# Queries and keys of block attention by a seven-product block scheme, in a fused Macaron layer

## The chip, the cores and the metric

The kernel runs on one core of a Trainium2 chip. Its metric is the device time of one execution in microseconds (us). The kernel before was run three times: 1013.26, 1014.03 and 1014.54 us, median 1014.03 us. A further execution was taken with the hardware profiler; all durations below come from that one.

A core has four computing engines that run their own queues of instructions: TensorE (PE; its weight loads are shown apart as PEld), VectorE (DVE), ScalarE (ACT) and GpSimd (POOL). SyncE (SP) issues most of the transfers between the main memory and the core. An engine takes its instructions in the order in which they stand in its queue, and waits on semaphores where an operand is not there yet.

## The reference, cut to what matters

The layer takes 2048 tokens of 1024 features in float32 and does

```python
x = x + 0.5 * ffn(layernorm(x))      # routed scales, +-1 weights
x = x + attn(layernorm(x))
x = x + 0.5 * ffn(layernorm(x))
```

The attention is the part in which the change lies:

```python
x = conv1d(inputs, conv_w, taps=3, 1024 -> 768) + conv_b
q, k, v = split(x, 3)                             # 256 features each
# 16 blocks of 128 tokens
qh = einsum('btd,dhe->bthe', q, wq) + bq          # 16 heads of 64
kh = einsum('btd,dhe->bthe', k, wk) + bk
vh = einsum('btd,dhe->bthe', v, wv) + bv
scores = einsum('bqhe,bkhe->bhqk', qh * scale, kh), causal
o = softmax(scores) @ vh
out = (einsum('bqhe,hed->bqd', o, wo) + bo) @ proj_w + proj_b
```

For the queries, `wq` is a matrix of 256 x 1024; so is `wk` for the keys. The depth of 256 is two times the 128 rows of TensorE.

## The kernel before

**Stages.** The kernel runs five stages one after the other: the first feed-forward part (0 to about 215 us of the span), the convolution (to 453.9 us), the attention (to about 846 us, its end mixed with the start of the last part) and the second feed-forward part with the stores. The convolution is written as a minimal-filtering scheme over two halves of the tokens. For each half, `conv_ends` and then `conv_middle` go over six column blocks `w` of 128 output features. In `conv_middle`, each `w` has two product groups on TensorE (`cv`, tiles `cv_{half}_{w}_{0,1}`, each 32 matmul records of 128x256, L475). Their weights `u` (k = 1 to 4) are computed from the three taps `g` by VectorE in `taps` (L465 to L471). There is one buffer for each `k`, so the weights for `w+1` can only be written when the products of `w` that read that buffer are done, and the next product group cannot begin before its weights are there. VectorE then combines the results into `y4` (L540 to L549), which SP stores to `qkv_dram` (L550). Before `conv_middle(1)`, the program asks for the first group of q, k and v (`load_qkv(0)`, L667) and the weights `wv`, `wq`, `wk` (L668).

**Attention.** The tokens are taken in four groups `g` of 512 (four blocks of 128), and each group goes over eight pairs of heads `hp` (128 columns). That gives 32 steps `(g, hp)`, and five stages that are pipelined over steps: at turn `i` the program emits `stage_qkv` of step `i`, `stage_softmax` of step `i-1`, `stage_transpose` of `i-2`, `stage_values` of `i-3` and `stage_wo` of `i-4`.

- `stage_qkv` computes q and k of a pair of heads as a 128x512 block each: two accumulating matmuls over the two halves of depth (L732; a float32 matmul shows as two records), then one VectorE instruction that adds the bias and moves the block out of PSUM (L741, L743). At `hp` 0 and 4 it first computes the values of four pairs (L716; 16 records), moved out by ScalarE and VectorE in turn (L724, L726).
- `stage_softmax`: eight matmuls for the scores (`sc`, L753), a ScalarE copy (L763), a GpSimd causal select (L765), a VectorE maximum (L775), four exponentials with sums on ScalarE (L778), a reciprocal and a scaling on VectorE (L785, L786); all twice, for the two heads.
- `stage_transpose` (`pt`, L794), `stage_values` (`ao`, L807) and `stage_wo` (`acc`, L824) follow. `stage_proj` (`pp`, L843) comes once per group.

PSUM has two banks of 128x512 for each of four kinds. The kind `mm` serves the values, q and k, the projection and the feed-forward products.

**Order.** The text order gives the priority. A planner in the framework moves instructions against each other within each engine's queue by its own estimates, unless they are pinned (`pin`, `keep_in_program_order`) or stand in a manual part. So the queue order is fixed when the program is built, and the hardware follows it. The q, k, v loads of group `g+1` are issued at `hp` 0 of group `g`, into one pool of two buffers (`qkvp`). The residual rows `xr` are loaded at `hp` 1, get `proj_b` added by GpSimd (L709), and live in one ring of eight buffers (`rring`) that the rows `xf` of the second feed-forward part use too.

Of the kernel before, what the change touches and what calls it, by code (L numbers as in the profile page):

```python
# [9 lines left out]
F32 = mybir.dt.float32  # L10
# [3 lines left out]
ALU = mybir.AluOpType  # L14
# [3 lines left out]
P = 128  # L18
NB = 512
# [5 lines left out]
def kernel(  # L25
# [22 lines left out]
    nc = tc.nc  # L48
# [15 lines left out]
    def pool(stack, name, bufs, **kw):  # L64
        return stack.enter_context(tc.tile_pool(name=name, bufs=bufs, reuse_waits="tile", **kw))
# [36 lines left out]
    def pin(ins):  # L102

        tc.keep_in_program_order(ins)
# [524 lines left out]
    with ExitStack() as ph:  # L629
        work = pool(ph, "work1", 2, side="right")  # L630
        ffn = Ffn("f1", work, xnp, 0, NT, lambda t: x1[t], next_x, norm_x2, transpose_x2, beside)
        with tc.manual_schedule():
            begin(ffn, work)
        for dst, src in ((conv_b_sb, conv_b), (bq_sb, bq), (bk_sb, bk), (bv_sb, bv), (bo_sb, bo)):
            tc.keep_in_program_order(nc.gpsimd.dma_start(out=dst, in_=src))
        ffn.run()
# [13 lines left out]

    b2 = ctx.enter_context(ExitStack())
    aw = pool(b2, "aw", 1, side="right")
    qkvp = pool(b2, "qkvp", 2, side="right")
    qkvs = {}

    def load_qkv(g):
        qkvs[g] = qkvp.tile([P, NW, NB], F32, name=f"qkv_{g}", tag="qkv")
        half, at = divmod(g * NB, TH)
        for w in range(NW):
            nc.sync.dma_start(out=qkvs[g][:, w, :], in_=qkv_dram[half][w][:, ds(at, NB)])  # L660
# [6 lines left out]
    load_qkv(0)  # L667
    wv_sb, wq_sb, wk_sb = (load_rows(aw, a, n, HE) for a, n in ((wv, "wv_sb"), (wq, "wq_sb"), (wk, "wk_sb")))  # L668
    conv_middle(1, mp)
# [3 lines left out]
    b3 = ctx.enter_context(ExitStack())  # L673
    f2 = ctx.enter_context(ExitStack())
    rring = pool(b3, "rring", 8)
    rows, x3 = {}, {}

    def load_rows2(t):
        if t in rows:
            return  # L680
        rows[t] = rring.tile([P, D], F32, name=f"xf_{t}", tag="x")
        nc.sync.dma_start(out=rows[t], in_=x3[t])
# [4 lines left out]
    with ExitStack() as ph:  # L687
# [3 lines left out]
        load_qkv(1)  # L691
# [6 lines left out]
        vhs, qks, prs, pTs, oTs, accs = {}, {}, {}, {}, {}, {}  # L698

        def stage_qkv(g, hp):  # L700
            if hp == 0 and g > 0 and g + 1 < NG:
                load_qkv(g + 1)
            if hp == 1:
                for t in range(g * BPG, (g + 1) * BPG):
                    rows[t] = rring.tile([P, D], F32, name=f"xr_{t}", tag="x")
                    nc.sync.dma_start(out=rows[t], in_=x2[t])
            if 3 <= hp < 3 + BPG:
                xt = rows[g * BPG + hp - 3]
                pin(nc.gpsimd.tensor_tensor(xt, xt, projb_sb, ALU.add))  # L709
# [18 lines left out]
            got = []  # L728
            for n, (w_sb, first) in enumerate(((wq_sb, 0), (wk_sb, WC))):
                pq = bank("mm", [P, NB], f"pq_{g}_{hp}_{n}")  # L730
                for c in range(WC):
                    nc.tensor.matmul(  # L732
                        pq,
                        lhsT=w_sb[:, c, ts(hp, P)],
                        rhs=qkvs[g][:, first + c, :],
                        start=(c == 0),
                        stop=(c == WC - 1),
                    )
                h = ap2.tile([P, NB], F32, name=f"qk_{g}_{hp}_{n}", tag=f"qk{n}")
                if n == 0:  # L740
                    nc.vector.tensor_scalar(h, pq, bq_sb[:, hp : hp + 1], QSCALE, ALU.add, ALU.mult)  # L741
                else:
                    nc.vector.tensor_scalar(h, pq, bk_sb[:, hp : hp + 1], None, ALU.add)  # L743
                got.append(h)
            qks[g, hp] = got

        def stage_softmax(g, hp):
            qh, kh = qks.pop((g, hp))
# [88 lines left out]
        def stage_proj(g):  # L837
            o2T = accs.pop(g)
            for b in range(BPG):
                for h in range(NH2):  # L840
# [9 lines left out]
                    xt = rows[g * BPG + b][:, ts(h, NB)]  # L850
# [3 lines left out]
                nc.sync.dma_start(out=x3[t], in_=rows.pop(t))  # L854

        stages = (stage_qkv, stage_softmax, stage_transpose, stage_values, stage_wo)
        ended, parts = None, []
        for i in range(len(steps) + len(stages)):
            for n, stage in enumerate(stages):
                if 0 <= i - n < len(steps):  # L860
                    stage(*steps[i - n])
                if n == 0 and i == len(steps) - 1:

                    b2.close()
                    work = pool(f2, "work2", 2, side="right")
                    ffn = Ffn("f2", work, work, 0, NT, lambda t: rows[t], load_rows2, store, lambda t: None, lambda t: None)
                    parts = ffn.fill()
                if n == 1 and ended is not None:
                    stage_proj(ended)
                    ended = None  # L870
                if n in (1, 3) and i >= len(steps) and parts:
                    parts.pop(0)()
            last = i - (len(stages) - 1)
            if 0 <= last < len(steps) and steps[last][1] == NHP - 1:
                ended = steps[last][0]
# [5 lines left out]
    b3.close()  # L881
# [53 lines left out]
```

## Time and profile before

| What | Value |
|---|---|
| median of three runs | 1014.03 us |
| profiled execution, its own time | 1014.76 us |
| span of that execution | 1013.0 us |
| TensorE busy | 984.3 us (97%) |
| VectorE busy | 665.6 us (66%) |
| ScalarE / GpSimd busy | 388.4 / 239.4 us |
| attention groups 1, 2, 3 (480 to 768 us), each 96 us: TensorE / VectorE busy | 95.5 / 55.6, 95.9 / 53.6, 95.9 / 53.6 us |
| convolution, second half (332 to 456 us): TensorE / VectorE busy | 123.5 / 76.0 us of 124 |
| TensorE granted clock | 0.999 |

In a line of the profile, L732 is line 732 of the kernel; `out<-in` names the tiles, then come the shape and the number of records. In the groups by line, the first pair of numbers is the busy time in us and the mean duration of one record in ns; the second says how long the engine was idle just before, and who ended most of that idle time. In the lists in order of time, the first two numbers are the start and the duration in us, and square brackets give an idle time and its releaser. Matmuls overlap, so the distance between starts says what one costs in a stream, not its duration.

### The profile page before, as it was taken

The page shows a single profiled execution, that of the slowest core. Times are in us where ns is not written, and L with a number is a line of the kernel's source. Part 1 is how long each engine was busy: PE and PEld are TensorE (multiplying, and loading weights), DVE is VectorE, ACT ScalarE, POOL GpSimd, SP SyncE. Part 2 cuts the span into 40 slices and gives each one's busy share as a digit, 9 for nine tenths or more (in the row PEclk, how much of TensorE's full clock was granted, in tenths as well). Part 3 has the DMA queues.
Part 4 walks back from the last instruction along what each step waited for, and adds up shares of the span by engine and source line. Part 5 has one row for each costly group of instructions (what it writes and reads, how often), then busy time and mean ns, then how long its engine had stood idle before and what let it go on. Part 6 is the DMA issues. An engine that isn't in the chain of part 4 may idle for free.

```text
span 1013.0 us, 14588 instructions
## 1 busy us (share of the span) xinstructions
PE 984.3 (97%) x5420; PEld 694.8 (69%) x5420; DVE 665.6 (66%) x1243; ACT 388.4 (38%) x1074; POOL 239.4 (24%) x335
## 2 busy tenths in 40 slices
PE   5999999999999999999999999999999999899997
PEld 3778888888888888884555455545554555677776
DVE  4888887748978537756656545655565556767664
ACT  3566665410110110114445424533462552545440
POOL 3554543300000000002312211221031312543421
PEclk9999999999999999999999999999999999999999
DMA  8767554698643786217020041013003207756421
GB/s 248 221 179 210 177 169 133 226 360 294 217 158 125 226 297 213 94 46 287 1 63 1 11 156 63 1 63 104 1 1 124 73 12 208 187 147 164 106 83 63
DMA packets 39705, 139.68 MB, mean 138 GB/s; under 512 B 4617, under 2 KB 5641, under 8 KB 38610
## 3 DMA queue, kind: packets, MB, share of 16 engines
q1 hardware_dynamic: 34528, 121.65, 33.6%
q0 software_dynamic: 5088, 17.06, 9.0%
q8 instruction: 43, 0.70, 0.3%
q14 instruction: 28, 0.23, 0.1%
q10 hardware_dynamic: 18, 0.04, 0.0%
HBM read 81.84 MB, written 40.11 MB: 120 GB/s over the span
## 4 chain that ended last, share of the span: by engine, by line
PE 39%; issue 38%; DVE 10%; DMA 6%; POOL 6%; ACT 1%; POOLq 0%; DVEq 0%
PE pm_f L286 15%; PE cv L475 7%; PE ce L475 4%; POOL xr L709 3%; DMA xf<-x 3%; DMA out_dram<-xf 2%; PE pp L843 2%; PE tr_f L199 2%; DVE st_f L157 2%; POOL p L765 2%; PE acc L824 1%; PE tr L398 1%; PE lgp_f L207 1%; PE is_f L250 1%; PE pq L732 1%
## 5 line engine op out<-in xcount | busy, mean ns | idle before, releaser
L286 PE MATMUL pm_f<-sw,y_f 128*128 128x512 f32 x1024 | 265.4, 407 | 0.2 <-DVE x L296 0.2
L286 PEld LDWEIGHTS pm_f<-sw,y_f 128*128 128x128 f32 x1024 | 185.9, 190 | 40.6 <-DVE x L296 0.4
L475 PE MATMUL cv<-v,u 128*128 128x256 f32 x768 | 166.3, 379 | 0.3 <-DVE u L467 0.3
L475 PEld LDWEIGHTS cv<-v,u 128*128 128x128 f32 x768 | 145.8, 190 | 20.4 <-PE cv L475 0.7
L765 POOL TENSOR_SCALAR_AFFINE_SELECT p<-p 128x512 f32<-128x512 f32 x64 | 39.7, 644 | 507.8 <-ACT p L763 507.8
L778 ACT ACTIVATE p<-p,anm 128x128 f32<-128x128 f32 x256 | 99.0, 388 | 17.5 <-DVE anm L775 17.5
L264 POOL TENSOR_TENSOR y_f<-xnT_f,y_f 128x512 fp32r<-128x512 f32 x64 | 81.3, 1288 | 66.1 <-ACT y_f L263 65.3
L475 PE MATMUL ce<-v,g 128*128 128x256 f32 x384 | 84.3, 380 | 0.9 <-ACT m L489 0.9
L763 ACT COPY p<-sc 128x512 f32<-128x512 f32 x64 | 34.3, 588 | 127.6 <-PE sc L753 127.5
L475 PEld LDWEIGHTS ce<-v,g 128*128 128x128 f32 x384 | 72.4, 190 | 12.1 <-ACT m L489 2.3
L775 DVE TENSOR_REDUCE anm<-p 128x4 f32<-128x512 f32 x64 | 40.9, 680 | 49.5 <-POOL p L765 49.5
L824 PE MATMUL acc<-oT,wo_sb 128*128 128x512 f32 x128 | 67.7, 617 | 0.4 <-DVE oT L816 0.4
L295 DVE TENSOR_TENSOR pm_f<-pm_f,os_f 128x512 f32<-128x512 f32 x64 | 44.4, 693 | 27.9 <-PE pm_f L286 27.3
L732 PE MATMUL pq<-qkv,wq_sb 128*128 128x512 f32 x128 | 60.4, 593 | 0.0
L732 PE MATMUL pq<-qkv,wk_sb 128*128 128x512 f32 x128 | 60.1, 592 | 0.0
L843 PE MATMUL pp<-pw_sb,o2T 128*128 128x512 f32 x128 | 57.6, 600 | 0.4
L716 PE MATMUL pv<-wv_sb,qkv 128*128 128x512 f32 x128 | 56.5, 593 | 0.0
L778 ACT ACTIVATION_READ_ACCUMULATOR p<-p,anm 128x1 f32 x256 | 48.0, 187 | 0.0
L753 PEld LDWEIGHTS sc<-qk,qk 64*128 64x128 f32 x512 | 31.1, 187 | 23.7 <-issue 22.2
L786 DVE TENSOR_TENSOR p<-p,asum 128x512 f32<-128x512 f32 x64 | 45.6, 713 | 2.2
L200 ACT COPY xnT_f<-tr_f 128x512 f32<-128x512 f32 x60 | 32.5, 589 | 37.9 <-PE tr_f L199 36.1
L732 PEld LDWEIGHTS pq<-qkv,wk_sb 128*128 128x128 f32 x128 | 24.3, 190 | 30.6 <-issue 28.7
(134 smaller groups left out, 1440.9 us busy)
## 6 DMA issues: line engine op xcount, KB each, us to landing
g<-in_conv_w_dram SPq DMA_DIRECT2D x60, 512.0 KB, 4.1
win<-xw SPq DMA_DIRECT2D x16, 528.0 KB, 2.7
xl<-win SPq DMA_DIRECT2D x8, 1056.0 KB, 7.4
x<-in_x_dram SPq DMA_DIRECT2D x16, 512.0 KB, 3.8
x<-hbias POOLq DMA_DIRECT2D x16, 512.0 KB, 4.9
x<-x SPq DMA_DIRECT2D x16, 512.0 KB, 4.1
xr<-x SPq DMA_DIRECT2D x16, 512.0 KB, 6.5
x<-xr SPq DMA_DIRECT2D x16, 512.0 KB, 3.9
```

Of the source, the lines that this page charges most:

```text
L264: nc.gpsimd.tensor_tensor(yl, y, yh.bitcast(F32), ALU.subtract)
L286: nc.tensor.matmul(pm, lhsT=y[:, n, c, :], rhs=sw[:, c, ts(h, NB)], start=(c == 0 and n == 0), stop=(c == DC - 1 and n == 1),)
L295: nc.vector.tensor_tensor(pm, pm, o, ALU.mult)
L475: nc.tensor.matmul(acc.rearrange("p (t q) -> p t q", q=QT), lhsT=uk[:, c, :], rhs=V[half, k][:, :, c, :], start=(c == 0), stop=(c == DC - 1),)
L716: nc.tensor.matmul(pv, lhsT=qkvs[g][:, 2 * WC + c, ts(b, P)], rhs=wv_sb[:, c, ts(half, NB)], start=(c == 0), stop=(c == WC - 1),)
L732: nc.tensor.matmul(pq, lhsT=w_sb[:, c, ts(hp, P)], rhs=qkvs[g][:, first + c, :], start=(c == 0), stop=(c == WC - 1),)
L765: nc.gpsimd.affine_select(out=p, in_=p, pattern=[[0, BPG], [-1, P]], compare_op=ALU.is_ge, fill=NEG_INF, base=0, channel_multiplier=1,)
L775: nc.vector.tensor_reduce(nmax, p, AX.X, ALU.max, negate=True)
L778: nc.scalar.activation(p[:, b, :], p[:, b, :], AF.Exp, bias=nmax[:, b : b + 1], accum_out=asum[:, b : b + 1],)
L786: nc.vector.tensor_tensor(p, p, asum.unsqueeze(2).broadcast_to([P, BPG, P]), ALU.mult)
L824: nc.tensor.matmul(accs[g][m], lhsT=wo_sb[:, hp, ts(m, P)], rhs=oT, start=(hp == 0), stop=(hp == NHP - 1),)
L843: nc.tensor.matmul(pp, lhsT=o2T[:, m, ts(b, P)], rhs=pw_sb[:, m, ts(h, NB)], start=(m == 0), stop=(m == WC - 1),)
```

## The change

Before, q (or k) of two neighbouring pairs of heads `2m`, `2m+1` takes 2 x 2 = 4 matmuls of 512 columns, which is 8 block products of 128 x 128 by 128 x 256 tokens: two heads-pairs x two halves of tokens x two halves of depth. The change computes the same four blocks from seven such products, by Strassen's scheme in Winograd's form.

- `seven_weights` (once for `wq`, once for `wk`): four VectorE instructions build the sums of the weight blocks, in a new tile `s_q` or `s_k` and in place. Before it, ScalarE multiplies `wq` by the scale in place (two instructions), and GpSimd does so for `bq`. They stand before `conv_middle(1)` in the text.
- `seven_inputs` (for each group, once for q and once for k): four VectorE instructions of 128x256 build the sums of the token blocks, one of them in place in the loaded q, k, v tile.
- `seven` (one unit for each two steps and each of q, k): four products into two `mm` banks; a ScalarE copy and four VectorE instructions on what they gave; then three more products, written over the places that have been read, each followed by a VectorE instruction that adds it and the bias into the result. At an even `hp` the k unit of the current two steps runs, at an odd `hp` the q unit of the next two. The first q unit runs before the loop.
- The order of the stages within a turn is written out anew: loads, softmax, projection, values of v, first four products, `stage_wo`, the last three products, transpose, values.
- Pools: the two q, k, v buffers become two pools of one (`qkv0`, `qkv1`), and `qkv1` is taken after the memory of the convolution is given back. The residual rows get a ring of their own with five buffers (`aring`); the rows of the second feed-forward part get theirs (`rring`, eight) after the attention's memory is released. The rows `xr` are loaded at `hp` 5 instead of 1, and GpSimd adds `proj_b` at turn `i - 7`.

The diff, cut to its core:

```diff
+        tc.keep_in_program_order(nc.gpsimd.tensor_scalar(bq_sb, bq_sb, QSCALE, None, ALU.mult))
...
-    qkvp = pool(b2, "qkvp", 2, side="right")
+    qkv0 = pool(b2, "qkv0", 1, side="right")
...
+    def seven_weights(w_sb, name):
+        s = aw.tile([P, 3, NHP // 2, P], F32, name=f"s_{name}")
+        (a11, a21), (a12, a22) = (
+            [w_sb.rearrange("p c (n m e) -> p c n m e", m=2, e=P)[:, c, :, m, :] for m in range(2)] for c in range(2)
+        )
+        s1, s2, s4 = (s[:, n, :, :] for n in range(3))
+        nc.vector.tensor_tensor(s1, a21, a22, ALU.add)
+        nc.vector.tensor_tensor(s2, s1, a11, ALU.subtract)
+        nc.vector.tensor_tensor(a21, a11, a21, ALU.subtract)
+        nc.vector.tensor_tensor(s4, a12, s2, ALU.subtract)
+        return dict(p1=a11, p2=a12, p3=s4, p4=a22, p5=s1, p6=s2, p7=a21)
...
+    for c in range(WC):
+        nc.scalar.mul(wq_sb[:, c, :], wq_sb[:, c, :], QSCALE)
+    sevens = [seven_weights(w_sb, n) for w_sb, n in ((wq_sb, "q"), (wk_sb, "k"))]
     conv_middle(1, mp)
...
-    rring = pool(b3, "rring", 8)
...
+        qkv1 = pool(b2, "qkv1", 1, side="right")
+        tp = pool(b2, "tp", 1, side="right")
+        aring = pool(ph, "aring", 5)
+        load_qkv(1, qkv1)
...
+        def seven_inputs(g, n):
+            x = qkvs[g][:, n * WC : n * WC + 2, :].rearrange("p c (h t) -> p c h t", h=2)
+            (b11, b12), (b21, b22) = ([x[:, c, h, :] for h in range(2)] for c in range(2))
+            t = tp.tile([P, 3, NB // 2], F32, name=f"t_{g}_{n}", tag=f"t{n}")
+            t2, t3, t4 = (t[:, j, :] for j in range(3))
+            nc.vector.tensor_tensor(b12, b12, b11, ALU.subtract)
+            nc.vector.tensor_tensor(t2, b22, b12, ALU.subtract)
+            nc.vector.tensor_tensor(t3, t2, b11, ALU.subtract)
+            nc.vector.tensor_tensor(t4, b21, t2, ALU.subtract)
+            ts_[g, n] = dict(p1=b11, p2=b21, p3=b22, p4=t4, p5=b12, p6=t2, p7=t3)
+
+        def seven(g, pair, n):
...
+            xy, zv = (bank("mm", [P, 2, NB // 2], f"qk_{g}_{pair}_{n}_{j}") for j in range(2))
+            px, py, pz, pv = xy[:, 0, :], xy[:, 1, :], zv[:, 0, :], zv[:, 1, :]
...
+            for dst, p in ((px, "p1"), (py, "p6"), (pz, "p7"), (pv, "p5")):
+                product(dst, p)
+            nc.scalar.copy(c11, px)
+            nc.vector.tensor_tensor(c12, py, c11, ALU.add)
+            nc.vector.tensor_tensor(c21, pz, c12, ALU.add)
+            nc.vector.scalar_tensor_tensor(c22, pv, b2, c21, ALU.add, ALU.add)
+            nc.vector.tensor_tensor(c12, pv, c12, ALU.add)
+            yield
+            for dst, p, c, bias in ((px, "p2", c11, b1), (pz, "p4", c21, b2), (py, "p3", c12, b1)):
+                product(dst, p)
+                nc.vector.scalar_tensor_tensor(c, dst, bias, c, ALU.add, ALU.add)
+            yield
...
-            for n, (w_sb, first) in enumerate(((wq_sb, 0), (wk_sb, WC))):
-                pq = bank("mm", [P, NB], f"pq_{g}_{hp}_{n}")
-                for c in range(WC):
-                    nc.tensor.matmul(
...
-                if n == 0:
-                    nc.vector.tensor_scalar(h, pq, bq_sb[:, hp : hp + 1], QSCALE, ALU.add, ALU.mult)
-                else:
-                    nc.vector.tensor_scalar(h, pq, bk_sb[:, hp : hp + 1], None, ALU.add)
...
+        for n in range(2):
+            seven_inputs(0, n)
+        for _ in seven(0, 0, 0):
+            pass
...
+            at(stage_loads, 0)
...
+            at(stage_softmax, 1)
+            if i == len(steps):
+                b2.close()
+                rring = pool(f2, "rring", 8, side="right")
...
+            at(stage_v, 0)
+            unit = (stage_qk(i) if i < len(steps) else None) or iter(range(2))
+            next(unit)
+            at(stage_wo, 4)
+            next(unit)
+            at(stage_transpose, 2)
+            at(stage_values, 3)
+            if i < len(steps):
+                g, hp = steps[i]
+                if hp in (5, 6) and g + 1 < NG:
+                    seven_inputs(g + 1, hp - 5)
```

## The prediction

> **What bounds the kernel now.** I read the engines' busy shares first.
>
> ```profile
> PE 984.3 (97%) x5420; PEld 694.8 (69%) x5420; DVE 665.6 (66%) x1243; ACT 388.4 (38%) x1074; POOL 239.4 (24%) x335
> ```
>
> TensorE is the bound over the whole span, and VectorE is busy for two thirds. Next I read TensorE in order of time through one attention step without values.
>
> ```profile
> 501.19 1.16 PE L753 MATMUL sc<-qk,qk 64*128 64x128 f32 x16
> 502.28 1.09 PE L794 MATMUL pt<-ident,p 128*128 128x128 f32 x8
> 503.21 1.02 PE L824 MATMUL acc<-oT,wo_sb 128*128 128x512 f32 x2
> 504.17 1.09 PE L807 MATMUL ao<-pT,vh 128*64 128x128 f32 x16
> 505.19 1.12 PE L824 MATMUL acc<-oT,wo_sb 128*128 128x512 f32 x2
> 506.15 1.88 PE L732 MATMUL pq<-qkv,wq_sb 128*128 128x512 f32 x4
> 507.87 1.88 PE L732 MATMUL pq<-qkv,wk_sb 128*128 128x512 f32 x4
> 509.68 1.16 PE L753 MATMUL sc<-qk,qk 64*128 64x128 f32 x16
> ```
>
> No line has square brackets: TensorE never waits, and a step lasts 509.68 - 501.19 = 8.49 us. Eight 512-wide records take 506.15 to about 509.6, 3.43 us, 0.43 each. That is what the seven products replace.
>
> VectorE's list across the convolution's second half shows how little room that stage has.
>
> ```profile
> 374.63 1.23 DVE L465 TENSOR_TENSOR u<-g,g 128x1024 f32<-128x1024 f32 x1 [3.36 <-PE cv L475]
> 378.08 1.22 DVE L466 TENSOR_TENSOR u<-u,g 128x1024 f32<-128x1024 f32 x1 [2.23 <-PE cv L475]
> 379.56 1.22 DVE L467 TENSOR_TENSOR u<-u,g 128x1024 f32<-128x1024 f32 x1
> 381.70 1.22 DVE L469 SCALAR_TENSOR_TENSOR u<-g,g 128x1024 f32<-128x1024 f32 x1
> 384.99 1.22 DVE L470 SCALAR_TENSOR_TENSOR u<-g,u 128x1024 f32<-128x1024 f32 x1 [2.07 <-PE cv L475]
> ```
>
> The next weights wait in turn for products to free their buffers (the brackets), and are ready by 380.8, 4 us before TensorE wants them at 384.8, where the products that the last of these lines waits for are done. VectorE's idle time here is not free time in its queue. The transfers issued in the same microseconds (second number: KB; last: median us to landing):
>
> ```profile
> wq_sb<-in_wq_dram SPq DMA_DIRECT2D x1, 1024.0 KB, 10.3
> ```
>
> The seam to the attention, in order of time over all engines, and two later transfers:
>
> ```profile
> 453.85 7.03 PE L716 MATMUL pv<-wv_sb,qkv 128*128 128x512 f32 x16
> ...
> 457.00 0.62 DVE L549 SCALAR_TENSOR_TENSOR y<-m,m 128x256 f32<-128x256 f32 x1
> ...
> 457.65 0.32 SPq L550 DMA_DIRECT2D qkv<-y  x1
> ```
>
> ```profile
> qkv<-y SPq DMA_DIRECT2D x1, 512.0 KB, 3.2
> ```
>
> ```profile
> qkv<-qkv SPq DMA_DIRECT2D x6, 256.0 KB, 4.8
> ```
>
> The values of group 0 start on TensorE the moment the convolution ends (453.85), and hide VectorE's last `y` operations and the store. Last, TensorE after idle time, at the program's start and in the second feed-forward part:
>
> ```profile
> 24.77 8.36 PE L286 MATMUL pm_f<-sw,y_f 128*128 128x512 f32 x24
> ```
>
> ```profile
> 868.17 0.33 PE L238 MATMUL rt_f<-ident,rhl_f 128*128 128x128 f32 x1 [2.34 <-DVE rhl_f L231]
> 868.25 2.12 PE L286 MATMUL pm_f<-sw,y_f 128*128 128x512 f32 x8
> ```
>
> **The change part by part.** I resolved which semaphores each instruction of the changed queues waits for, and set durations from the rows above. All is summed against the profiled execution's 1014.76 us (span 1013.0), 0.07% over the median of 1014.03.
>
> *a. Weight sums in the convolution.* In the changed VectorE queue the eight operations of `seven_weights` stand right after the L469 that began at 381.70, and ahead of L465, L466, L467 of the next `w`. The first waits for ScalarE's two scalings of `wq`, which wait for the load: issued at 372.15, landed 382.45. A 128x512 ScalarE copy goes by at 0.52, so 128x1024 takes 1.04: 384.5. Eight 128x512 operations at 0.68 (the 0.69 row of L786): 390.0. Then L465, L466, L467 (1.14 apart, 1.22 the last) and three small ones between, 4.7 together: 394.7. TensorE wants this at 384.8, so it stands for **10.0**. If the load were no obstacle, the eight would start at 382.8: 8.1. If it lands in 13.0 us, as two `g` loads beside it did: 12.7.
>
> *b. Start of the attention.* The changed TensorE queue begins with the first q unit, not the values; p6 needs the sums L727, L728 of VectorE, which come after L549 (457.62), so four products are done by about 459. In VectorE's queue, between that unit's `c21` and `c22`, stands L727 for **group 1**, the in-place difference. It waits for the loads of group 1, these on SP for completion of the last `y` store: 457.65 + 3.2 = 460.9, and landing 3.9 to 4.8 later: 465.2. Behind it: `c22`, `c12` and three closing adds (L752 to L757), 0.4 to 0.48 each: 467.6. The values wait in TensorE's order for the closing adds (PSUM places), and start at 467.7 where before they started at 453.85. 3.0 of that is the unit's own products, so **10.8** is lost. Without the group 1 wait it would be 5.6; with the landing of `wq` (10.3) instead, 14.
>
> *c. Ramp.* k unit, scores and first softmax have no other TensorE work beside them; before, there were gaps of 0.55 here at most. I take **+2.5** (1 to 4), some five handovers of 0.5.
>
> *d. Loads of groups 2 and 3.* One buffer each now, so a load starts only after the last k unit of the group that held it. L727 for it stands in VectorE's queue ahead of the next step's maxima; it is reached some 2.5 after the last product, and the load lands 3.9 to 4.8 after. With the maxima wait the exponentials and all of that step: **+3.3** for both (0 if a slack elsewhere covers it, 6 at the landing's worst).
>
> *e. The plain step.* Seven 128x256 products: 65 `cv` records (128x256) spanned 14.03, 0.216 each, two per product: 3.02 for a unit, 0.41 less than 3.43, at most 13.1 over 32 steps. But p3, the last product, waits for VectorE's chain, which in the queue follows the maxima of the same turn. From the start of the scores: 2.52 to the first maximum (467.68 to 470.20), two maxima 1.24, two adds 0.92, `c22` 0.40, reciprocal 0.12, add 0.35, scaling 0.64, closing add 0.48, with a 0.07 handover 6.74. TensorE's own work before p3, waiting included, comes to about 6.7 to 6.8. So both end together, and the narrow products add changes of shape, at about 0.1 each (8.49 against 8.13 for the sum of pieces). p3 at 6.82, itself 0.43, then values 1.02 and a change 0.1: period 8.37, 0.12 better. With about 0.3 on the eight steps with values: **-5** (from -13, VectorE hidden, to +5, rows from PSUM dearer).
>
> *f. TensorE after the two stands of 10.* In the row at 24.77, after 4.33 us of waiting a little earlier, 24 records take 8.36 where the 8 records at 868.25 take 2.12 (24: 6.4; by starts the gap is 2.2). After 2.34 us of idle time nothing was slower. Twice 2.2: **+4.4** (0 to 4.4). The trace's granted clock gives no slower figure there. The Trainium skill's page "TensorE: Matmul & The Clock Gate", section "What's actually happening", says an idle window of about 3.4 us halves the rate until a like window was busy. The rows at 24.77 and 868.25 fit it in sign; by its figure each stand would cost an estimated 1.7 and the sum would be 1.0 lower.
>
> *g. Rows of the second feed-forward part.* They no longer queue for `xr` slots; the gaps at its start (0.81, 0.61, 2.34) go at most: **-2** (-3.8 to 0). The later `xr` loads, GpSimd's adds and the smaller `aring` have several steps' time and cost nothing; if they are late, the projection is, once per group.
>
> Sum: 10.0 + 10.8 + 2.5 + 3.3 - 5 + 4.4 - 2 = +24.0: 1038.8, **1039 us**.
>
> **The rivals.** *Mild.* The loads land before their turn: a 8.1, b 5.6, c 1, d and f 0, e -8, g -3: +3.7, 1018.5. For it: VectorE idles a third. Against: the `y` store cannot be issued before 457.6. *VectorE sets the step.* If the operations that read PSUM cost 0.6 rather than 0.46 (0.75 against 0.69 is what a scalar operand adds at 512), five in the chain add 0.7; less slack, a step lasts 8.7 and e becomes +6: 1050. Against: VectorE was busy only 5.6 of 8.49. *Other side: TensorE's stream alone sets the step.* If the pieces flow without changes of shape, 7.72 us per step: 0.77 x 32 = -24.6; with a 8.1, b 5.6, c 1, g -3.8: 1001. It decides from 0.91 us per step on with my stalls (29.0 / 32), from 0.34 with those lower ends. Against: no step of before goes without these 0.36 us, and 6.74 is VectorE's. That the change doesn't do what it says is out: the changed queue holds seven products per unit and 32 units.
>
> **How the numbers follow.** Mine 0.60 (1028 to 1050), mild 0.15, VectorE 0.16, other side 0.09. The range takes in mild (with c at nothing and g at its end, -3.8: 1016.7) and VectorE's with b at its upper end (1050 + 3.2, and d some higher: 1054), and leaves the other side out. A measurement of this kernel tells about 0.2% from no change. Faster by more: 0.09; within: 0.02 (between mild and the other side); slower: 0.89.
>
> **What would show it.** Right: in the changed profile `cv` stands for 8 to 12 us before the second group of w = 1, with VectorE as its releaser; a second gap near 460 to 480, ended by VectorE after a DMA; scores of plain steps 8.3 to 8.5 apart, VectorE near 6.5 of it; two gaps of 1 to 3 at the changes of group. Wrong: no gap in `cv` (an earlier landing); scores under 8.1 apart (e, the other side) or over 8.6 (VectorE); values starting soon after the convolution (b).

## The result and the profile after

The changed kernel took 1054.33 us (median of five runs, 1050.41 to 1055.66) against 1014.06 us for the kernel before (five runs beside them, 1013.26 to 1014.54). The ratio is 1.0392, with an interval of 1.0371 to 1.0414: **3.9% slower**. The profiled execution took 1054.33 us itself, with a span of 1052.5 us, 39.5 us more than the 1013.0 us before. The differences below are between these two spans.

The page's first part, engines' busy times, changed kernel:

```profile
PE 993.4 (94%) x5612; PEld 740.3 (70%) x5612; DVE 725.5 (69%) x1443; ACT 403.0 (38%) x1108; POOL 242.2 (23%) x336
```

TensorE is busy 9.1 us longer, although it has less to multiply, and idle for 59 us where it was 29. The half clock shown further down is about as large: by the granted clock, the four stretches at half rate from 388 us on (near 388, 470, 552 and 907 us) lengthen TensorE's work by an estimated 8.7 us. VectorE has 200 more instructions and 60 us more work.

TensorE's waits over the whole span (waiting line, releaser; total us, times, longest):

```profile
PE cv L475 <- DVE u L467: 9.1, 2, 8.8
PE qk L745 <- DVE qk L753: 6.9, 8, 4.7
PE qk L745 <- DVE qk L750: 6.3, 4, 3.0
...
PE rt_f L238 <- DVE rhl_f L231: 5.1, 6, 2.3
...
PE qk L745 <- DVE t L728: 3.4, 1, 3.4
```

Four of the five lines are new; that of `rt_f`, in the second feed-forward part, was there before with 4.7 us. Now TensorE in order of time at the places of the new ones: the convolution, the start of the attention, and late in groups 0 and 1.

```profile
370.92 13.98 PE L475 MATMUL cv<-v,u 128*128 128x256 f32 x64
393.71 1.62 PE L475 MATMUL cv<-v,u 128*128 128x256 f32 x3 [8.82 <-DVE u L467]
...
465.35 0.59 PE L745 MATMUL qk<-qkv,wq_sb 128*128 128x256 f32 x2
469.37 0.70 PE L745 MATMUL qk<-t,s_q 128*128 128x256 f32 x2 [3.43 <-DVE t L728]
...
477.39 1.22 PE L745 MATMUL qk<-t,wq_sb 128*128 128x256 f32 x2 [4.67 <-DVE qk L753]
...
551.45 0.70 PE L745 MATMUL qk<-qkv,wq_sb 128*128 128x256 f32 x2 [2.99 <-DVE qk L750]
551.99 1.55 PE L843 MATMUL pt<-ident,p 128*128 128x128 f32 x8
...
652.27 0.70 PE L745 MATMUL qk<-qkv,wq_sb 128*128 128x256 f32 x2 [2.84 <-DVE qk L750]
```

Why VectorE released them so late stands in its own list. The first line opens the eight weight sums, behind which L465 for the next weights begins only at 389.30. The second is the in-place difference of group 1 at the start of the attention, the third that of group 2 late in group 0:

```profile
384.02 0.69 DVE L678 TENSOR_TENSOR s_q<-wq_sb 128x512 f32<-128x512 f32 x1 [1.32 <-ACT wq_sb L688]
...
476.19 0.42 DVE L727 TENSOR_TENSOR qkv<-qkv 128x256 f32<-128x256 f32 x1 [3.86 <-DMA qkv<-qkv]
...
546.57 0.49 DVE L727 TENSOR_TENSOR qkv<-qkv 128x256 f32<-128x256 f32 x1 [1.58 <-DMA qkv<-qkv]
546.98 2.56 DVE L729 TENSOR_TENSOR t<-t,qkv 128x256 f32<-128x256 f32 x1
...
549.80 1.26 DVE L824 TENSOR_REDUCE anm<-p 128x4 f32<-128x512 f32 x2
550.99 0.41 DVE L750 TENSOR_TENSOR qk<-qk,qk 128x256 f32<-128x256 f32 x1
```

Both differences wait for their load, and what waits behind them in the queue is what TensorE needs: the maxima of the softmax, and L750, whose result frees the place of the next product. The granted clock of TensorE (start and end of the stretch, its length, TensorE's busy time and records, then the clock; the last two numbers are the transfers' share and rate) tells the rest of what a wait costs:

```profile
388.00:388.50 0.50, 0.00 (x0) 1.00 0.00 0
388.50:389.00 0.50, 0.00 (x0) 0.53 0.00 0
...
396.00:398.00 2.00, 2.00 (x6) 0.50 0.57 231
...
398.50:399.00 0.50, 0.50 (x3) 0.73 0.50 90
399.00:400.00 1.00, 1.00 (x7) 1.00 0.79 311
```

TensorE's last product before the wait ended at 384.9. At about 388.5 the clock halved, and it came back at about 398.7, when TensorE had been working again for 5.0 us. Those 5.0 us of work are worth half, a loss of 2.5 us behind the wait of 8.8.

The plain step, TensorE in order of time, changed kernel:

```profile
573.11 1.16 PE L802 MATMUL sc<-qk,qk 64*128 64x128 f32 x16
...
576.03 1.88 PE L873 MATMUL acc<-oT,wo_sb 128*128 128x512 f32 x4
577.75 0.59 PE L745 MATMUL qk<-qkv,wq_sb 128*128 128x256 f32 x2
578.18 0.49 PE L843 MATMUL pt<-ident,p 128*128 128x128 f32 x3
578.79 0.70 PE L745 MATMUL qk<-t,wq_sb 128*128 128x256 f32 x2
579.33 0.71 PE L843 MATMUL pt<-ident,p 128*128 128x128 f32 x5
579.87 0.61 PE L745 MATMUL qk<-qkv,s_q 128*128 128x256 f32 x2
580.41 1.09 PE L856 MATMUL ao<-pT,vh 128*64 128x128 f32 x16
581.44 1.16 PE L802 MATMUL sc<-qk,qk 64*128 64x128 f32 x16
```

No wait, 581.44 - 573.11 = 8.33 us against 8.49. So the plain step gained 0.16, and the steps with values lost it again. Over such a step, at `hp` 4, the scores are 16.28 us apart (752.60 to 768.88) where they were 15.36 (709.88 to 725.24).

### The profile page after: what moved, and what is told of

It reads as the page before. It is cut to its first block, busy times and chain, and to the rows that moved or that the text cites. A ratio compares the mean times of both kernels' runs of the same rounds, so it can differ in the third digit from the quotient of the medians.

```text
span 1052.5 us, 15239 instructions
## 1 busy us (share of the span) xinstructions
PE 993.4 (94%) x5612; PEld 740.3 (70%) x5612; DVE 725.5 (69%) x1443; ACT 403.0 (38%) x1108; POOL 242.2 (23%) x336
## 4 chain that ended last, share of the span: by engine, by line
issue 56%; PE 26%; DVE 6%; POOL 6%; DMA 3%; ACT 2%; POOLq 0%; DVEq 0%; ACTq 0%; SPq 0%
PE pm_f L286 18%; POOL xr L924 3%; PE tr_f L199 2%; POOL p L814 2%; DMA xf<-x 1%; PE pp L892 1%; DVE st_f L157 1%; PE lgp_f L207 1%; PE is_f L250 1%; DMA out_dram<-xf 1%; PE tr L398 1%; DVE xnT_f L261 1%; DVE pm_f L295 1%; PE acc L873 1%; ACT xn_f L170 0%
## 5 line engine op out<-in xcount | busy, mean ns | idle before, releaser
L286 PE MATMUL pm_f<-sw,y_f 128*128 128x512 f32 x1024 | 268.9, 411 | 0.2 <-DVE x L296 0.2
L286 PEld LDWEIGHTS pm_f<-sw,y_f 128*128 128x128 f32 x1024 | 188.2, 193 | 41.0 <-DVE x L296 0.4
L475 PE MATMUL cv<-v,u 128*128 128x256 f32 x768 | 169.1, 383 | 9.1 <-DVE u L467 9.1
L873 PE MATMUL acc<-oT,wo_sb 128*128 128x512 f32 x128 | 60.8, 596 | 0.3 <-DVE oT L865 0.3
L775 PEld LDWEIGHTS pv<-wv_sb,qkv 128*128 128x128 f32 x128 | 23.9, 193 | 30.8 <-issue 26.4
L275 ACT ACTIVATE os_f<-po_f 128x512 f32<-128x512 f32 x64 | 34.9, 594 | 24.1 <-DVE pm_f L295 12.7
L892 PEld LDWEIGHTS pp<-pw_sb,o2T 128*128 128x128 f32 x128 | 23.2, 189 | 29.5 <-issue 23.2
L802 PE MATMUL sc<-qk,qk 64*128 64x128 f32 x512 | 42.1, 289 | 0.0
```

Of the source, the lines that this page charges most:

```text
L286: nc.tensor.matmul(pm, lhsT=y[:, n, c, :], rhs=sw[:, c, ts(h, NB)], start=(c == 0 and n == 0), stop=(c == DC - 1 and n == 1),)
L475: nc.tensor.matmul(acc.rearrange("p (t q) -> p t q", q=QT), lhsT=uk[:, c, :], rhs=V[half, k][:, :, c, :], start=(c == 0), stop=(c == DC - 1),)
L775: nc.tensor.matmul(pv, lhsT=qkvs[g][:, 2 * WC + c, ts(b, P)], rhs=wv_sb[:, c, ts(half, NB)], start=(c == 0), stop=(c == WC - 1),)
L802: nc.tensor.matmul(sc[j][:, b, :], lhsT=qh[ts(j, DH), ts(b, P)], rhs=kh[ts(j, DH), ts(b, P)], start=True, stop=True,)
L873: nc.tensor.matmul(accs[g][m], lhsT=wo_sb[:, hp, ts(m, P)], rhs=oT, start=(hp == 0), stop=(hp == NHP - 1),)
L892: nc.tensor.matmul(pp, lhsT=o2T[:, m, ts(b, P)], rhs=pw_sb[:, m, ts(h, NB)], start=(m == 0), stop=(m == WC - 1),)
```

## The experiments

For all kernels below, a table first. Each ratio is to runs of the kernel before on the same chip, whose medians were 1014.0 to 1015.2 us. "Attention" is the time from the first record after the convolution to the first product `pm_f` of the second feed-forward part, both read from TensorE's list of the profiled execution. What lies behind `pm_f` takes the same in both kernels (165.9 us before, 166.6 after), and the stages ahead of the attention end at 451.9 to 455.9 us in all kernels but the changed one and e2, from one execution to another. So this length is a better measure of the attention than the whole time. It is read from one execution of each kernel, though, and holds what the half clock cost there. By the granted clock, that lengthened TensorE's work in the attention by an estimated 4.5 us in the changed kernel, 7.8 in e1, 4.9 in e2, 1.6 in e4, 8.2 in e5, 11.7 in e6, 1.7 in e8 and 3.4 in e10; in the other kernels no stretch at half rate falls into it.

| Kernel | median us | ratio to before, interval | attention us | plain step us |
|---|---|---|---|---|
| before | 1014.06 | | 393.2 | 8.49 |
| changed | 1054.33 | 1.0392 (1.0371 to 1.0414) | 420.6 | 8.33 |
| e1 weight sums late | 1044.41 | 1.0291 (1.0268 to 1.0313) | 423.2 | |
| e2 token sums pinned | 1045.29 | 1.0301 (1.0277 to 1.0324) | 411.4 | |
| e3 both, values first | 1027.80 | 1.0124 (1.0099 to 1.0149) | 404.7 | 8.33 |
| e4 as e3, wide products | 1025.91 | 1.0108 (1.0088 to 1.0128) | 404.7 | 8.74 |
| e5 one order pinned | 1047.38 | 1.0335 (1.0311 to 1.0359) | 426.7 | 8.57 |
| e6 as e5, wide | 1047.66 | 1.0336 (1.0314 to 1.0357) | 428.8 | |
| e7 another order held | 1025.65 | 1.0118 (1.0098 to 1.0137) | 404.3 | 8.03 |
| e8 as e7, wide | 1023.79 | 1.0100 (1.0081 to 1.0120) | 402.8 | 8.34 |
| e9 values split | 1016.13 | 1.0019 (1.0007 to 1.0030) | 394.6 | 8.03 |
| e10 as e9, wide | 1019.12 | 1.0042 (1.0027 to 1.0057) | 399.0 | |
| e11 start filled | 1018.06 | 1.0044 (1.0028 to 1.0059) | 395.3 | |
| e12 start and tail filled | 1014.04 | 0.9997 (0.9979 to 1.0015) | 392.1 | |

"Wide" means the 512-column products of before, two per block and without any sums, in the pools, the loads and the stage order of its partner.

### Are the two long waits what the prediction says? (e1, e2)

The theory: the weight sums stand in VectorE's queue where the next weights `u` are wanted (a), and the in-place difference, put ahead in the queue, holds up everything behind it while its load is on the way (b, d). The rival: the waits hide something else that would take their place.

e1 moves the scaling of `wq` and the eight weight sums behind the `y` operations of `w` = 4, and pins them there:

```diff
+            if w + 2 == NW and late is not None:
+                late()
...
-    for c in range(WC):
-        nc.scalar.mul(wq_sb[:, c, :], wq_sb[:, c, :], QSCALE)
-    sevens = [seven_weights(w_sb, n) for w_sb, n in ((wq_sb, "q"), (wk_sb, "k"))]
-    conv_middle(1, mp)
+    def weight_sums():
+        for c in range(WC):
+            pin(nc.scalar.mul(wq_sb[:, c, :], wq_sb[:, c, :], QSCALE))
+        sevens.extend(seven_weights(w_sb, n) for w_sb, n in ((wq_sb, "q"), (wk_sb, "k")))
+
+    conv_middle(1, mp, weight_sums)
```

> The eight weight sums on VectorE and the two scalings of wq on ScalarE are moved to the end of the convolution's second half (after the y operations of w = 4), where VectorE stands idle for 5 us; nothing else is changed. My theory (term a with its part of f): the wait of 8.8 us in the products and the slower TensorE behind it (320 records in 71.8 instead of 69.0 us) go, some 11.5 us: about 1043. Rival (the sums cost VectorE time wherever they stand, and the seam to the attention pays it): the first q unit starts later by up to the 5.5 us of the sums, about 1048 or more.

It took 1044.41 us. The wait of `cv` is gone, the clock stays at 1.00 from 372 to 400 us, and the convolution ends at 453.93, 11.4 us earlier: the wait of 8.8 and the slow stretch behind it. The attention is longer by 2.6 us; in it the clock was at 0.50 twice at the start, and once more from 642 to 649 us, behind a wait of 2.84 us that left the clock at 1.00 in the changed kernel. The theory holds for a, and for the half-clock part of f.

e2 keeps the four token sums of groups 1 to 3 at their place in the text:

```diff
-            nc.vector.tensor_tensor(b12, b12, b11, ALU.subtract)
...
+            put = pin if g else lambda ins: ins
+            put(nc.vector.tensor_tensor(b12, b12, b11, ALU.subtract))
...
```

> The sums of token blocks of groups 1 to 3 (lines 727 to 730) are held at the place in VectorE's queue where the text has them, five or six turns later than the planner put them; nothing else is changed. My theory (terms b and d): the wait of VectorE for the loads goes at three places, 4 to 5 us at the start of the attention and 3 to 5 us each in groups 0 and 1, together 12 to 13: about 1041. Rival (the waits there are VectorE's own chain, and the load only ends last by chance): at most 3 us, 1051 or more.

It took 1045.29 us, 9.0 less. The values start 9.9 us after the convolution and not 13.9, and both waits of nearly 3 us in the groups are gone. That is the theory's mechanism, but less than expected from it. Pinned, the sums cost about 0.6 us a group: the two steps in which they stand came out at 8.71 and 9.19 us.

### What is left when the waits are gone? (e3, e4)

e3 does both, and computes the values of group 0 ahead of the first q unit, as before. e4 has e3's order with the wide products.

```diff
             seven_inputs(0, n)
+        stage_v(0, 0)
         for _ in seven(0, 0, 0):
...
-            at(stage_v, 0)
+            if i:
+                at(stage_v, 0)
```

```diff
+            w_sb, first = ((wq_sb, 0), (wk_sb, WC))[n]
...
+            for m, b in enumerate((b1, b2)):
+                pq = bank("mm", [P, NB], f"qk_{g}_{pair}_{n}_{m}")
+                for c in range(WC):
+                    nc.tensor.matmul(
...
+                nc.vector.tensor_scalar(h[:, m, :], pq, b, None, ALU.add)
+                yield
```

> Both edits, and the values of group 0 ahead of the first q unit as in the kernel before. My theory: conv 11.5, start 18.5 less a ramp of some 4 (14.5), loads 8 go: about 1020, and what is left over the kernel before (some 6) is the ramp, the plain steps and the steps with values, which cost 0.6 a group more than before and not less. Rival (without the stalls the seven products show their gain of up to 0.41 a step, which the stalls hid): 1005 to 1012.

> As the third kernel of this group, but a unit is four accumulating 512-wide matmul pairs and two VectorE moves, as before the change; weight sums and token sums are left out. So it has the order of stages, the pools and the loads of the changed kernel without the seven products. My theory (VectorE's chain and the changes of shape eat the saved 0.41 a step): 1012 to 1019, within 4 us of the third kernel on either side. Rival (the seven products are worth their 13 us of TensorE): slower than the third kernel by 8 to 13.

1027.80 and 1025.91 us: e3 did not come down to what was expected of it, and e4 shows why. **Without a single one of the seven products the attention is as long as with them** (404.7 us), 11.5 us over the kernel before. What remains is the price of the new order of the stages, with its pools and loads; their shares were not measured one by one. TensorE in one plain step of e4:

```profile
553.00 1.16 PE L775 MATMUL sc<-qk,qk 64*128 64x128 f32 x14
554.08 1.98 PE L723 MATMUL qk<-qkv,wk_sb 128*128 128x512 f32 x4
...
559.33 1.04 PE L816 MATMUL pt<-ident,p 128*128 128x128 f32 x8
560.30 0.48 PE L775 MATMUL sc<-qk,qk 64*128 64x128 f32 x2
560.72 1.09 PE L829 MATMUL ao<-pT,vh 128*64 128x128 f32 x16
```

The planner pulled two score records ahead of `ao`. The two take 0.42 us by the starts, and the fourteen that are left still take 1.08, as much as all sixteen in one piece (1.09). The split costs 0.42 us a step. In the changed kernel's step above it is the transposes that are split, 0.61 + 0.54 us for what takes 0.87 in one piece (next experiment). The tail costs too. The q units run two steps ahead, so the last steps have nothing beside them, and in e3 two of the last `ao` wait 2.0 and 1.3 us for ScalarE's copies of `pT`.

### Whole pieces (e5 to e8)

e5 pins all TensorE instructions of the attention in one order, with no piece split: scores, values, four products, `acc`, three products, `pt`, `ao`. e6 has the same with wide products.

```diff
-                nc.tensor.matmul(dst, lhsT=a[p][:, pair, :], rhs=b[p], start=True, stop=True)
+                pin(nc.tensor.matmul(dst, lhsT=a[p][:, pair, :], rhs=b[p], start=True, stop=True))
...
-                    nc.tensor.transpose(pt[:, b, :], p[:, b, :], ident)
+                    pin(nc.tensor.transpose(pt[:, b, :], p[:, b, :], ident))
```

> The third kernel, with TensorE's instructions of the attention held in the order of the text: scores, (values), first four products, output products, last three products, transposes, values of attention; each piece whole. The three adds after the last products are written behind all three. Theory (the stalls apart, what is left over the kernel before is TensorE's changes of shape and split pieces): a step without values is 1.09 + 1.83 + 1.82 + 1.39 + 0.97 + 1.02 = 8.1 us instead of 8.3 to 9.2, a group some 93 instead of 97, about 1012 in all. Rival (VectorE's chain sets the step): steps of 8.3 or more and 1022 to 1028.

> The same clean order with the kernel before's 512-wide products in place of the seven, sums left out. Theory (seven products save TensorE time, 0.41 a step, when nothing else is in the way): 8 to 12 us slower than the kernel run beside it, near 1021. Rival (VectorE's extra operations cost what the products save): equal within 2 us.

Both came out far above what was expected, at 1047.4 and 1047.7 us. TensorE's waits of e5:

```profile
PE ao L865 <- ACT pT L855: 15.5, 30, 3.1
PE pv L784 <- DVE vh L794: 7.3, 4, 1.9
```

With `ao` right behind `pt`, each step waits for ScalarE to copy the transposes out (0.29 us a plain step, 3.1 at the tail). The values in one piece need four banks where there are two, and wait for VectorE to empty them. Behind some of these waits the clock halved, which is the 8.2 us of half rate named above for e5. What looked like disorder in the planner's queue was partly cover for such waits.

e7 puts the last three products between `pt` and `ao`, splits the values at `hp` 4 around `acc`, and holds the order only in turns 4 to 31. e8 is e7 with wide products.

```diff
+            held[0] = 4 <= i < len(steps)
...
+                if i < len(steps) and i % NHP == PPV:
+                    stage_v(*steps[i], range(2))
+                    at(stage_wo, 4)
+                    stage_v(*steps[i], range(2, BPG))
...
             next(unit)
-            at(stage_wo, 4)
-            next(unit)
+            if i % NHP != PPV or i >= len(steps):
+                at(stage_wo, 4)
             at(stage_transpose, 2)
+            next(unit)
             at(stage_values, 3)
```

> The fifth kernel mended where its own order made new waits: transposes stand between the output products and the last three products (so that the values of attention no longer come right behind the transposes whose PSUM bank they need), the values of v at hp 4 stand half before and half after the output products, and the order is held in turns 4 to 31 only, so that the end of the attention is the planner's again. Theory (changes of shape, split pieces and waits for banks were the remainder): steps of 8.0 to 8.2 us, a group some 93 to 94 us, 1010 to 1015 in all, level with the kernel before. Rival (VectorE's or ScalarE's chain, which no order removes, sets the step): 8.3 and more, above 1020.

> The same with the 512-wide products of the kernel before and without the sums. Theory (the seven products are worth TensorE's 0.41 us a step in this order): steps of 8.4 to 8.6, 8 to 12 us slower than the kernel run beside it. Rival (they are worth nothing): equal within 2 us.

TensorE in a plain step of e7:

```profile
553.68 1.16 PE L818 MATMUL sc<-qk,qk 64*128 64x128 f32 x16
...
558.32 1.04 PE L859 MATMUL pt<-ident,p 128*128 128x128 f32 x8
559.19 0.60 PE L758 MATMUL qk<-qkv,wk_sb 128*128 128x256 f32 x2
...
560.68 1.09 PE L872 MATMUL ao<-pT,vh 128*64 128x128 f32 x16
561.71 1.16 PE L818 MATMUL sc<-qk,qk 64*128 64x128 f32 x16
```

561.71 - 553.68 = 8.03 us, without a wait; `pt` in one piece takes 0.87. Against the changed kernel's 8.33 this is about what the split transposes had cost (0.28 us by the rows). e8's step is 8.34, so the seven products save 0.31 us a plain step, of the 0.41 that the count of products gives. Yet e7 as a whole is not faster than e8, and its attention is 11.1 us longer than before, in spite of the shorter step. At `hp` 0, where the values were not split, TensorE waits:

```profile
535.20 3.70 PE L792 MATMUL pv<-wv_sb,qkv 128*128 128x512 f32 x8 [1.85 <-DVE vh L802]
```

### Handovers (e9 to e12)

e9 splits the values at `hp` 0 too, and does the in-place difference of the next group at `hp` 2 and 3, apart from the other sums. e10 is e9 with wide products.

```diff
-                if i < len(steps) and i % NHP == PPV:
+                if i < len(steps) and i % PPV == 0:
...
+                if hp in (2, 3) and g + 1 < NG:
+                    first_difference(g + 1, hp - 2)
```

> The seventh kernel with two mends: at hp 0, too, the values of v stand half before and half after the output products (there TensorE waited 1.85 us in each of three groups for a copy of v out of PSUM), and the in-place differences (line 727) are taken at hp 2 and 3, so that only three sums and not four stand before the maxima at hp 5 and 6. Theory: 1.5 and 0.7 us a group less, about 1019, and no more than level with the kernel before, since the start and the end of the attention still stand. Rival (the order has no more to give): within 2 us of the seventh kernel.

> The same with the 512-wide products and without the sums. Theory: 1.5 us a group less than the eighth kernel, about 1019; against the ninth it tells what the seven products are worth with all waits found so far mended: 3 to 6 us if each of the plain steps keeps its 0.32, nothing if the sums and the interleaved steps take it back.

1016.13 and 1019.12 us. The attention is 394.6 us with the seven products and 399.0 with the wide ones. Here, with the same order in both and no wait in the plain steps, the scheme is worth 3.0 us by the medians, though the two intervals still overlap (1.0007 to 1.0030 and 1.0027 to 1.0057). The 4.4 us between the two lengths say less: in e10's execution the clock was at 0.50 for 3.4 us near 487 and again near 815, an estimated 3.4 us of TensorE's work together, and in e9's nowhere in the attention. Its 0.31 us would be 9.9 over 32 steps; the rest is given back outside the plain steps. How it divides among the values, the sums and the ends wasn't measured.

e11 computes the second half of the values of group 0 in turns 0 and 1, where the ramp has gaps. e12 does that, and moves half of the projection of group 2 into the tail, beside the last `ao`.

```diff
-                if i < len(steps) and i % PPV == 0:
+                if i == PPV:
+                    at(stage_wo, 4)
+                elif i < len(steps) and i % PPV == 0:
...
+            if i in (0, 1):
+                stage_v(0, PPV, range(2 * i, 2 * i + 2))
```

```diff
-                stage_proj(ended)
+                stage_proj(ended, range(BPG if ended != NG - 2 else 2))
...
+            if i in (len(steps) + 1, len(steps) + 2):
+                stage_proj(NG - 2, [i - len(steps) + 1])
```

> The ninth kernel with the second half of the values of group 0 moved from turn 4 into turns 0 and 1, where TensorE waits for the first softmax and the first units. Theory (the ramp of the start, 3.8 us at the first values of attention, is TensorE without independent work): 2 to 4 us less than the ninth kernel, 1012 to 1014. Rival (the ramp is the chain of scores, softmax and units, and work put into it only delays the chain): equal or slower.

> The eleventh kernel with half of the projection of group 2 moved from turn 28 into turns 33 and 34, where the last units are done and TensorE waits for softmax. Theory (q units run two steps ahead, so that the end of the attention has 3 us less TensorE work beside the same chain): 2 to 3 us less than the eleventh, 1009 to 1012, so faster than the kernel before. Rival (the chain there is delayed by what is put into it): equal or slower than the eleventh.

e11 took 1018.06 us and gained nothing: its attention is 395.3 us, 0.7 over e9's. e12 took 1014.04 us, which is **level with the kernel before** (0.9997, 0.9979 to 1.0015), with an attention of 392.1 us. Work for the empty tail is worth 3.2 us by that length and 4.0 by the medians, more than the 2 to 3 expected, but the end below the kernel before that was expected with it did not come. With all the repairs the scheme breaks even; no version beat the kernel before. What e12 would take with wide products, and what its order for the tail would do for the kernel before, was not run.

## Why the prediction was right in direction and short in size

Direction and places were as predicted: the marks named were a wait of 8 to 12 us in `cv` (8.8), a gap near 460 to 480 ended by VectorE after a load (3.4 and 4.7), plain steps of 8.3 to 8.5 (8.33), and two gaps of 1 to 3 at the changes of group (3.0 and 2.8). The time lies at the very upper end of what the range was drawn to take in (1054), and outside the likeliest case's own (1028 to 1050). Term by term against the measured differences of the two profiled spans:

| Term | predicted | measured | read from |
|---|---|---|---|
| a weight sums | +10.0 | +8.8 | wait of `cv` |
| f half clock, convolution | +2.2 | +2.7 | 320 records in 71.8 us, 69.0 before; 11.5 in all |
| b start | +10.8 | +10.9 | values begin 13.9 after the convolution, less 3.0 of the unit |
| f half clock, values | +2.2 | +0.8 | 7.8 us for 16 records, 7.0 before |
| c ramp | +2.5 | +6.8 | rest of the 18.5 us until the fourth `ao` |
| d loads of groups 2, 3 | +3.3 | +7.6 | 4.5 and 3.1 over a group change without such a wait |
| e steps | -5 | +1.7, end of the attention -0.5 | three group lengths |
| g second feed-forward part | -2 | +0.7 | `pm_f` to the end |
| sum | +24.0 | +39.5 | |

- **a** was right in mechanism and nearly in size. ScalarE's scalings ended at 384.0 (estimate 384.5), and a sum came every 0.60 us, not 0.68, because neighbours overlap. e1 shows it.
- **b** was right to 0.1 us: the group 1 difference came 10.8 us after the convolution's end (estimate 11.3), and what stands behind it took a little longer. That the sum came so close is partly luck: the unit's last two products ran at half the clock there, 1.9 us (477.39 to 479.26) for what takes 1.1 later (490.33 to 491.39), and the prediction had put such time into f. e2 took 4.0 us of the start away by moving that difference.
- **f** is shown by the granted clock, which the trace of before did not show. The size was right in the convolution. At the start most slow products lay beside the wait for the load, where they cost nothing. The Trainium skill's page "TensorE: Matmul & The Clock Gate" ("What's actually happening") gives half rate after an idle window of about 3.4 us until such a window was busy, an estimated 1.7 us a stand. The runs agree in the factor, 0.50; the busy time until the return was 5.0 us, so 2.5 was lost. They also show half rate behind waits well under 3.4 us (last section).
- **d** failed in size. The step that failed is "reached some 2.5 after the last product", with the landing 3.9 to 4.8 after it and the maxima as the only work behind. The waits were 2.99 and 2.84 us. Behind the difference stand two more sums before the maxima and L750, and one of them has a row of 2.56 us where its like take 0.41 (L729 at the first wait, L730 at the second); the trace doesn't name the reason. VectorE's own wait for the landing was only 1.58 us at the first and 0.62 at the second, so this row is the larger part. Then the clock halved behind the first wait, for an estimated 1.7 us more. e2 removed both waits.
- **c** failed in size. Waits of TensorE between the first values and the fourth `ao` come to 2.1 us, about the 2.5 predicted. The other 4.7 us are not waits: scores and transposes go in many small pieces there, which was not priced. That these pieces are all of it wasn't shown.
- **e** is the step that failed in kind. The period was right (8.37 predicted, 8.33 measured), its reason wrong, so the agreement is luck. VectorE's chain does not set the step, since e7 runs the same operations, with the three closing adds together, in 8.03. The stream of TensorE sets it, and about 0.3 us of it went to the split transposes. The "about 0.3" gained at the eight steps with values was a loss instead: the one at `hp` 4 lost 0.92 us (16.28 against 15.36).
- **g** failed. The gaps remained, at 0.80, 0.61 and 2.3 us. The first is ended by VectorE's `rhl_f`, and VectorE's list shows what that chain had waited for: ScalarE's `ro_f`, not a load of the rows. Behind the gap of 2.3 the clock halved (last section), which made eight `pm_f` records 1.4 us longer; the measured +0.7 holds that.

```profile
891.27 0.16 DVE L226 RECIPROCAL rsum_f<-rsum_f 128x1 f32<-128x1 f32 x1 [2.80 <-ACT ro_f L225]
```

Of the rivals, the mild case fell, since the loads did not land before their turn. "VectorE sets the step" was priced at 1050, close to the outcome, but its mark, scores over 8.6 apart in plain steps, showed in a single step late in the attention (768.88 to 777.49, 8.61, with 0.40 us of waiting for VectorE). The other side, TensorE's stream alone, was right about what sets the step (8.03 in e7, not 7.72), but the stalls outweighed what that gains.

## What to carry to other kernels

Fewer multiplications in a TensorE-bound stage pay only as far as the stream stays in whole pieces, without waits: here the scheme's gain of 0.31 us a step was outweighed by one split piece (0.30 to 0.42) and by three places where its sums stood in an in-order queue ahead of urgent work. Price a new operation by what stands behind it in its queue, above all when it waits for a load, and add the half-clock time that can follow a wait of TensorE, here one of about 1.8 us already. To judge a scheme, run its order with the old products as well; only the pair tells the two prices apart.

## What the runs showed of the hardware

- The half clock can come late, and the length of the wait alone doesn't tell whether it comes. After the wait of 2.99 us the clock halved at about 552.4, when TensorE had been at work again for 0.9 us, and stayed so for 3.4 us. After the wait of 2.84 us in the same execution it did not halve at all; after the same wait in e1 it did, for 6.8 us. In the second feed-forward part a wait of 2.35 us was followed by 3.4 us at half the clock, and eight `pm_f` records took 3.54 us, where the kernel before took 2.12 behind a wait of 2.34. A wait of 1.86 us ahead of the values was followed by half rate all three times that it came in e6 (eight records in 5.40 us), the same wait in e7, three times too, not once (3.70). The stretches at half rate last 3.4, 6.8 or 10.2 us in all these traces, the one behind the last matmul apart. The windows of the changed kernel behind the wait of 2.99, then the changed kernel's rows at 907 us, and e6's first wait ahead of the values:

```profile
552.00:553.00 1.00, 1.00 (x8) 0.68 0.00 0
553.00:554.00 1.00, 1.00 (x5) 0.50 0.00 0
...
555.00:556.00 1.00, 1.00 (x3) 0.61 0.00 0
556.00:557.00 1.00, 1.00 (x17) 1.00 0.00 0
```

```profile
907.00 0.33 PE L238 MATMUL rt_f<-ident,rhl_f 128*128 128x128 f32 x1 [2.35 <-DVE rhl_f L231]
907.09 3.54 PE L286 MATMUL pm_f<-sw,y_f 128*128 128x512 f32 x8
```

```profile
538.36 5.40 PE L748 MATMUL pv<-wv_sb,qkv 128*128 128x512 f32 x8 [1.86 <-DVE vh L758]
```

- Cutting a group of small matmuls in two costs time: two of sixteen score records taken out cost 0.42 us, and eight transposes took 0.28 us more in two pieces than in one.
